# Attention and a looped mixture of experts: an earlier first load of w2, a longer lead of the given rows, nine fewer tiles turned by TensorE

## The chip, the cores and the metric

The kernel runs on one core of a Trainium2 chip, in one launch, in fp32. The metric is the device time of one execution in microseconds, as the median of repeated runs. The names of the engines in the profile: PE is TensorE (matmuls; PEld its weight loads), DVE is VectorE, ACT is ScalarE, POOL is GpSimd, SP is SyncE, which here only issues DMAs. A name with q (SPq) is an engine's sequencer, which issues and waits.

## The reference, cut to what matters

The input x is 2 sequences of 2048 tokens with 256 dimensions, 4096 tokens in all.

```
x = x + layernorm(attention(layernorm(x)))        # one head of 128, rotary positions
z = layernorm(x)
for _ in range(2):                                # LOOPS
    z_norm = rmsnorm(z) * norm_w
    scores = softmax(z_norm @ router_w)           # 8 experts
    the two largest scores, divided by their sum, are the weights of two experts
    z = z + sum over both: weight * ((silu(z_norm @ w1[e]) * (z_norm @ w3[e])) @ w2[e])
x = x + layernorm(z)                              # w1, w3: 256 x 512, w2: 512 x 256 per expert
```

The second loop's routing needs the first loop's results, token by token.

## The kernel before, in words

**Stages.** First the projections of x (to about 83 us in the profiled execution), then the attention (to about 410 us), then the experts: 71 tiles of 128 token rows for each loop, 142 in one sequence (a short end follows, in which the results of loop 1 are summed and normed). All the order of the work is written out by hand in Python, and each engine executes its own instructions in that order. An instruction that waits holds up everything behind it on its engine, and a DMA that waits holds up everything behind it on the queue that issues it.

**Attention.** A loop over `step` computes a block of scores in each step. For the first sequence (`EXCHANGED`) the exponentials are moved into turned blocks by DMAs on SP (`move_chunks`, L1449, tile `wall<-pr`, sixteen for each pair of query tiles) and VectorE turns them within blocks (`turn_chunks`, tile `pt`). In between, `extend(e)` (L1375 and on) works out for each expert the product of w2 with the router's weights: four DMAs on SP bring w2 into `wb`, four VectorE transposes make `wT`, eight small matmuls make `tp_e`. In the loop `p` numbers the pairs of query tiles and `a` runs from 0 to 7 within one; `p = -1` is the lead-in of the pipeline. `extend` is begun, which issues its four DMAs, at `a == NS - 3`, that is 5, of the pair before the one in which it is used.

**The expert tiles.** `slot(m, beside, size)` puts down the work around tile m. A tile passes these steps, each several slots apart:

- `gather` (GpSimd, indirect DMA): 128 rows of `zd` into `xg`, two tiles to a buffer. It needs the list `token`, which the routing ends with.
- `keep` (SP): a pair of tiles is written to DRAM, `xs<-xg`. `load` (SP): four DMAs bring it back with its blocks exchanged, `xb<-xs`. Both are left out for a *direct* tile.
- `turned`, two slots ahead of the matmuls: VectorE turns `xb` within blocks (`xT<-xb`). For a direct tile TensorE turns `xg` with two matmuls against the identity (`tp_x`, L1011) and ScalarE copies the result (L1012).
- `hidden`: eight records of matmul on TensorE, `p` (L1025), and ScalarE's silu, `a` (L1034). `gate`: VectorE's product `g` (L1039), and its DMA `gd<-g` on SP (L1044).
- `hidden_back`, once for two tiles: four DMAs `gb<-gd` on SP (L1051). `turn_hidden`: VectorE's `gT`. `mix`, five slots after `hidden`: the matmuls `py` (L1067).
- `give`: ScalarE's evacuation `y` (L1080), and GpSimd's indirect DMA to `given` (L1081), where each token finds its two rows.

The PSUM pool of `py` and `tp_x` has two banks; that of p has two for `p1` and three for `p3`.

**Which tiles are direct** is a list of ranges (loop, first, end), with NX = 71:

```
DIRECT = ((0, 54, NX), (1, 0, 2), (1, 12, 30), (1, 54, NX))
```

**Routing beside the tiles.** The tokens of a loop are in two groups, the first of 18 blocks of 128, the second of 14. `before` of a group of loop 1 first takes up the results of loop 0 (`logits`): `load_given` issues a DMA of 528 KB on SP for two blocks (L316, `given<-given`), `add_first` has ScalarE multiply the second rows (L337) and VectorE add the first rows to z (L338), `add_second` has GpSimd add the rest (L344). Then logits, softmax, the two largest, the positions and the lists follow, mostly on VectorE. Such a routine is a generator whose `yield` gives its cost in units. `advance` runs it beside the tiles with a budget of 16 or 17 units for each slot, in two halves, one ahead of `hidden` and `mix` and one behind them (SLOT = 16, HALF = 8). So a yield of 8 puts what comes behind it half a slot later.

Of the kernel before, what the change touches and what calls it, by code (L numbers as in the profile page):

```python
# [29 lines left out]
def attn_moe_kernel(  # L30
# [21 lines left out]
    E, _, F = w1.shape  # L52
# [13 lines left out]
    NX = TOP_K * T + E - 1  # L66
# [162 lines left out]
    def load_expert(e):  # L229
        a = ND * F  # L230
        for j, w in enumerate((w1, w3)):
            nc.sync.dma_start(
                out=wall[:, e, j * a : (j + 1) * a].rearrange("p (c f) -> p c f", c=ND),
                in_=by_dims(w[e]),
            )
        spread(wall[:, e, 2 * a :].rearrange("p (c d) -> p c d", c=NF)[:, :, :D], w2[e], NF)
# [33 lines left out]
    SLOT, HALF = 16, 8  # L270
# [5 lines left out]
    class Turn:  # L276
# [116 lines left out]
        def logits(self):  # L393

            n = self.n
            last = self.loop - 1
            nc.vector.tensor_copy(self.z[:, :, D:Z], raw[:, self.ts, :])
            y = {}
            yield SLOT
            for i in range(2):  # L400
                y[i] = self.load_given(last, i, nc.sync)
                yield HALF
            ms = rpool.tile([P, NM], F32, tag="fl_sd", name="ms")[:, :n]
            rms = rpool.tile([P, NM], F32, tag="fl_sh", name="rms")[:, :n]
            lg = self.lg.rearrange("p e t -> p t e")
            done, parts = 0, []

            for i in range(n // 2 + 5):
                if i + 2 < n // 2:
                    y[i + 2] = self.load_given(last, i + 2, nc.sync)  # L410
                if parts and parts[0][0] == i - 2:
                    _, part = parts.pop(0)
                    w = part.stop - part.start
                    nc.vector.tensor_tensor(
                        lg[:, part, :],
                        self.z[:, part, D:Z],
                        rms[:, part].rearrange("p (t o) -> p t o", o=1).to_broadcast([P, w, E]),
                        ALU.mult,
                    )

                    nc.vector.tensor_copy(self.z[:, part, D], rms[:, part])
                if 0 <= i - 3 < n // 2 and ((i - 3) % 3 == 2 or i - 3 == n // 2 - 1):
                    part = slice(done, 2 * (i - 2))
                    parts.append((i, part))
                    done = part.stop
                    w = part.stop - part.start
                    nc.vector.tensor_scalar(
                        ms[:, part], rms[:, part], 1.0 / D, RMS_EPS, ALU.mult, ALU.add
                    )
                    nc.gpsimd.tensor_tensor(rms[:, part], ms[:, part], neg_half[:, :w], ALU.pow)  # L430
                if 0 <= i - 2 < n // 2:
                    for t in range(2 * i - 4, 2 * i - 2):
                        sq = rpool.tile([P, D], F32, tag="sq", name="sq")
                        nc.scalar.activation(
                            sq, self.z[:, t, :D], AF.Square, accum_out=rms[:, t : t + 1]
                        )
                if 0 <= i - 1 < n // 2:
                    self.add_second(i - 1, y.pop(i - 1))
                if i < n // 2:
                    self.add_first(last, i, y[i])  # L440
                yield 6 if i >= n // 2 else 10 if self.g == 0 else 12
            assert not parts and not y

        def store(self, i):
# [493 lines left out]
    TURN = 2  # L938


    DIRECT = ((0, 54, NX), (1, 0, 2), (1, 12, 30), (1, 54, NX))
    BACK = 4
    LAG = 5

    class Job:


        def __init__(self, loop, i):
# [3 lines left out]
            self.first = self.second = None  # L952
            self.direct = any(l == loop and lo <= i < hi for l, lo, hi in DIRECT)

# [401 lines left out]
    NS = NT // 2  # L1356
    LEAD = NS + 1
    LATER = 6
    with tc.tile_pool(name="prob", bufs=6, **left) as pprob, tc.tile_pool(
# [44 lines left out]
        def score(u):  # L1404
            t, c = divmod(u, NKC)
            b, qi = divmod(t, NT)
            if c == 0:
                nms[t] = small.tile([P, NKC], F32, tag="m4", name="m4")
            sc[u] = ps_s.tile([P, KC], F32, tag="sc", name="sc")
            nc.tensor.matmul(  # L1410
                sc[u],
                lhsT=qkT[b][:, 0, qi * P : (qi + 1) * P],
                rhs=qkT[b][:, 1, c * KC : (c + 1) * KC],
                start=True,
                stop=True,
            )
            nc.vector.tensor_reduce(nms[t][:, c : c + 1], sc[u], AX.X, ALU.min)  # L1417
            if c == NKC - 1:
                nm = small.tile([P, 1], F32, tag="nm", name="nm")
                nc.vector.tensor_reduce(nm, nms[t], AX.X, ALU.min)  # L1420
                nms[t] = nm

        def exponents(u):
            t, c = divmod(u, NKC)
            if c == 0:
                s4s[t] = small.tile([P, NKC], F32, tag="s4", name="s4", bufs=6)
            p, i = divmod(t, QG)
            if i == 0:
                prs[p, c] = pprob.tile([P, QG, KC], F32, tag="pr", name="pr")
            nc.scalar.activation(  # L1430
                prs[p, c][:, i],
                sc.pop(u),
                AF.Exp,
                bias=nms[t],
                scale=-1.0,
                accum_out=s4s[t][:, c : c + 1],
            )
# [7 lines left out]
        def move_chunks(p, c):  # L1445

            pr = prs.pop((p, c))
            for a in range(4):
                nc.sync.dma_start(  # L1449
                    out=standing(p)[32 * c : 32 * (c + 1), :, a], in_=pr[32 * a : 32 * (a + 1)]  # L1450
                )
# [121 lines left out]
        for step in range(NS * NP + LEAD + LATER + 1):  # L1573
            u = chunks.get(step - NKC - 1)
            if u is not None and u // (NT * NKC) in EXCHANGED:
                t, c = divmod(u, NKC)
                p, i = divmod(t, QG)
                if i == QG - 1:
                    move_chunks(p, c)
            u = chunks.get(step - NKC)  # L1580
            if u is not None:
                exponents(u)
            p, a = divmod(step - LEAD - LATER, NS)
            if 0 <= p < NP:
                (turn_chunks if p // (NP // B) in EXCHANGED else transposes)(p, a)
            for gen in list(leaving):
                if next(gen, True):
                    leaving.remove(gen)
            if (p, a) >= (ROUTED + 1, 1):
                credit = min(credit, 0) + STEP  # L1590
                while credit > 0:
                    took = next(first, None)
                    if took is None:
                        break
                    credit -= took
                if credit > 0:
                    for m in itertools.islice(ahead, 1):
                        fetch_rows(m)
            u = chunks.get(step)
            if u is not None:  # L1600
                score(u)
            if a == 0 and 0 < p <= NP:
                values(p - 1, NS - 1)
                leaving.append(leave(p - 1))
                next(leaving[-1])
                if p == NP // B:

                    bigs[0].close()
                    rpool = ctx.enter_context(tc.tile_pool(name="route", bufs=1, **right))
                    spool = ctx.enter_context(tc.tile_pool(name="rows", bufs=2, **right))  # L1610
            if 0 <= p < NP:
                for g in WHEN.get(a, ()):
                    values(p, g)
            if a == NS // 2 and HELD <= p - NP // B + HELD < E:
                load_expert(p - NP // B + HELD)
                nc.gpsimd.tensor_copy(
                    extended(p - NP // B + HELD), ext[:, p - NP // B, :, :]
                )
            if a == NS - 3 and -1 <= p < E - 1:
                extending = extend(p + 1)  # L1620
                next(extending)
            elif 0 <= p < E and a < NS - 3:
                next(extending)
            e = p if p < NP // B else p - 1 - NP // B + HELD
            if (0 <= p < HELD or p > NP // B) and e < E:
                if a == 2:
                    scaling = scale_expert(e)
                    next(scaling)
                elif a == 5:
                    next(scaling)  # L1630
# [116 lines left out]
```

## Time and profile before

| | us |
|---|---|
| median of 3 runs | 1220.25 |
| lowest and highest of them | 1219.07, 1220.92 |
| profiled execution, its own time | 1223.01 |
| its span, first to last instruction | 1221.2 |
| mean granted TensorE clock, as a share of full speed | 0.981 |

The profile is of one execution. Of each engine it tells the busy time, for groups of equal instructions the count and mean duration, and for the idle time ahead of an instruction what ended it (its releaser). The chain of waits follows the execution back from its last instruction to what released each step. All times of day in what follows are microseconds from the span's start. Which wait counts must be read in the stretch where it lies: a busy share of the whole span is a mean over stages with different limits.

### The profile page before, as it was taken

What the parts mean: (1) busy time and instruction counts of PE and PEld (TensorE: products, weight loads), DVE (VectorE), ACT (ScalarE), POOL (GpSimd) and SP (SyncE); (2) the same over time, 40 slices, a digit from 0 to 9 for tenths busy, and PEclk for the clock granted to TensorE, in tenths of its full rate; (3) what the DMA queues carried; (4) which work ended last, traced back from release to release, by engine and by line L of the source; (5) the groups of instructions that cost most, each with busy time, mean ns of one, the idle gap of its engine ahead of it and who ended that gap; (6) DMA issues with size and microseconds to landing.
All of it is one profiled execution on the core that took longest, in us unless ns stands there. A gap on an engine that the chain in (4) does not pass through costs nothing.

```text
span 1221.2 us, 16498 instructions
## 1 busy us (share of the span) xinstructions
PE 1150.9 (94%) x4082; PEld 709.6 (58%) x4082; DVE 655.2 (54%) x1707; ACT 423.9 (35%) x967; POOL 627.1 (51%) x1011
## 2 busy tenths in 40 slices
PE   6986999899989799999999999998999999999985
PEld 4543666566766455555555566555666555566554
DVE  5645788767797368433333558224673333367314
ACT  4443333235545222222222642223522222244314
POOL 3560485555422444455444773554744554478573
PEclk9988999999999899999999999999999999999988
DMA  4715688725301588798877966588765897888755
GB/s 147 215 36 128 148 204 196 180 87 155 96 26 53 139 229 218 197 236 237 217 203 214 275 185 175 164 234 246 225 182 148 232 253 218 232 268 250 209 169 185
DMA packets 232169, 226.25 MB, mean 185 GB/s; under 512 B 83280, under 2 KB 179408, under 8 KB 232080
## 3 DMA queue, kind: packets, MB, share of 16 engines
q1 hardware_dynamic: 208592, 161.08, 48.6%
q0 software_dynamic: 20752, 60.97, 17.8%
q10 hardware_dynamic: 2736, 3.16, 0.8%
q8 instruction: 39, 0.64, 0.2%
q14 instruction: 50, 0.41, 0.1%
HBM read 123.82 MB, written 84.52 MB: 171 GB/s over the span
## 4 chain that ended last, share of the span: by engine, by line
PE 58%; DMA 4%; issue 2%; SPq 2%; DVE 1%; ACT 0%; POOL 0%; ACTq 0%; DVEq 0%; POOLq 0%
PE p L1025 37%; PE py L1067 19%; DMA given<-given 1%; PE tp_x L1011 1%; SPq L995 1%; DMA gd<-g 1%; DMA gb<-gd 1%; PE sum L917 1%; DMA xg<-zd,token 1%; SPq L1051 0%; DMA zd<-y 0%; DMA xs<-xg 0%; PE ps_l L665 0%; DVE ln_st L198 0%; DMA given<-y,to 0%
## 5 line engine op out<-in xcount | busy, mean ns | idle before, releaser
L1025 PE MATMUL p<-wall,xT 128*128 x1136 | 515.2, 597 | 6.7 <-ACT a L1034 5.0
L1025 PEld LDWEIGHTS p<-wall,xT 128*128 128x128 f32 x1136 | 212.7, 192 | 220.7 <-issue 210.0
L1081 POOL DMA_INDIRECT given<-y,to x142 | 143.9, 1013 | 301.5 <-ACT y L1080 212.2
L1067 PE MATMUL py<-wall,gT 128*128 x1136 | 274.2, 385 | 5.8 <-issue 5.8
L1067 PEld LDWEIGHTS py<-wall,gT 128*128 128x128 f32 x1136 | 217.4, 192 | 98.0 <-issue 70.5
L1039 DVE TENSOR_TENSOR g<-a,p 128x512 f32<-128x512 f32 x142 | 97.2, 685 | 270.3 <-issue 226.6
L1080 ACT ACTIVATE y<-py,rms 128x264 f32<-128x264 f32 (+1 forms) x142 | 67.5, 475 | 337.2 <-PE py L1067 318.7
L966 POOL DMA_INDIRECT xg<-zd,token x142 | 142.3, 1002 | 33.0 <-issue 24.3
L1034 ACT ACTIVATE a<-p,rms 128x512 f32<-128x512 f32 x142 | 97.3, 685 | 157.2 <-PE p L1025 106.1
L1410 PE MATMUL sc<-qkT 128*128 128x512 f32 x256 | 134.5, 620 | 11.9 <-ACT pr L1430 11.1
L263 DVE STREAM_TRANSPOSE gT<-gb 128x512 f32<-128x512 f32 x142 | 100.1, 706 | 67.4 <-DMA gb<-gd 66.6
L1482 PE MATMUL po<-pt,v 128*128 128x256 f32 x512 | 129.9, 388 | 1.9 <-DVE pt L1456 1.6
L1482 PEld LDWEIGHTS po<-pt,v 128*128 128x128 f32 x512 | 98.5, 194 | 53.6 <-issue 35.2
L1430 ACT ACTIVATE pr<-sc,nm 128x512 f32<-128x512 f32 x128 | 87.6, 690 | 97.2 <-DVE nm L1420 63.4
L1417 DVE TENSOR_REDUCE m<-sc 128x1 f32<-128x512 f32 x128 | 87.7, 686 | 37.4 <-PE sc L1410 37.1
L185 POOL TENSOR_TENSOR rds<-rs_v,neg_half 128x2 f32<-128x2 f32 (+1 forms) x24 | 19.8, 824 | 95.3 <-DVE rs_v L184 94.7
L1410 PEld LDWEIGHTS sc<-qkT 128*128 128x128 f32 x256 | 45.6, 197 | 31.8 <-ACT pr L1430 20.6
L1456 DVE STREAM_TRANSPOSE pt<-wall 128x512 f32<-128x512 f32 x64 | 43.8, 685 | 9.3 <-DMA wall<-pr 8.4
L263 DVE STREAM_TRANSPOSE xT<-xb 128x256 f32<-128x256 f32 x88 | 35.7, 407 | 20.8 <-DMA xb<-xs 20.8
L1253 PE MATMUL pm<-wqkvT,hT 128*128 128x392 f32 x128 | 46.5, 507 | 0.0
L243 POOL TENSOR_SCALAR wall<-wall,nwp 128x1024 f32<-128x1024 f32 x16 | 45.8, 2863 | 0.2
L1469 PE MATMUL tp_p<-ident,pr 128*128 128x128 f32 x256 | 40.2, 276 | 5.0 <-ACT pr L1430 3.6
(270 smaller groups left out, 1133.6 us busy)
## 6 DMA issues: line engine op xcount, KB each, us to landing
gd<-g SPq DMA_DIRECT2D x142, 256.0 KB
gb<-gd SPq DMA_DIRECT2D x284, 128.0 KB
wall<-pr SPq DMA_DIRECT2D x128, 128.0 KB
xs<-xg SPq DMA_DIRECT2D x44, 257.0 KB
xb<-xs SPq DMA_DIRECT2D x176, 64.0 KB
given<-given SPq DMA_DIRECT2D x16, 528.0 KB
wall<-in_L_ffn_w SPq DMA_DIRECT2D x16, 512.0 KB
z<-zd POOLq DMA_DIRECT2D x32, 256.0 KB
```

The lines of the kernel that those rows point to most:

```text
L263: nc.vector.transpose(out=dst.rearrange("p c (a t) -> p a c t", t=32), in_=src.rearrange(f"p (a {columns}) -> p a c d", a=4, c=dst.shape[1]),)
L966: i = nc.gpsimd.indirect_dma_start(out=self.xg[:, k, :], out_offset=None, in_=zd[self.loop][: (SPLIT if self.i < WHOLE else T) * P, :], in ...
L1025: nc.tensor.matmul(ps, lhsT=self.xT[:, c, :], rhs=wall[:, bass.ds(self.e, 1), o : o + F].rearrange("p o f -> p (o f)"), start=(c == 0), st ...
L1034: nc.scalar.activation(self.a, p1, AF.Silu, scale=self.rms)
L1039: nc.vector.tensor_tensor(g, self.a, self.p3, ALU.mult)
L1067: nc.tensor.matmul(py[:, :w], lhsT=self.gT[:, f, :], rhs=wall[:, bass.ds(self.e, 1), o : o + w].rearrange("p o d -> p (o d)"), start=(f == 0),
L1080: nc.scalar.mul(y, self.py, self.rms)
L1081: i = nc.gpsimd.indirect_dma_start(out=given[self.loop], out_offset=bass.IndirectOffsetOnAxis(ap=self.row(self.turn.to), axis=0), in_=y, i ...
L1410: nc.tensor.matmul(sc[u], lhsT=qkT[b][:, 0, qi * P : (qi + 1) * P], rhs=qkT[b][:, 1, c * KC : (c + 1) * KC], start=True, stop=True,)
L1417: nc.vector.tensor_reduce(nms[t][:, c : c + 1], sc[u], AX.X, ALU.min)
L1430: nc.scalar.activation(prs[p, c][:, i], sc.pop(u), AF.Exp, bias=nms[t], scale=-1.0, accum_out=s4s[t][:, c : c + 1],)
L1482: nc.tensor.matmul(pos[p], lhsT=vn[p * QG // NT][:, 2 * g + j, :HD], rhs=pt[:, j, :], start=(g == 0 and j == 0), stop=(g == NS - 1 and j = ...
```

## The change

Three places, in the words of the code:

1. `logits`: one more `yield HALF` between the first two loads of given rows and the first sum, and a cost of 11 instead of 12 for each step of the second group. The two loads keep their place, and the work behind them is put down half a slot later.
2. `DIRECT`: nine tiles (3 + 2 + 4) are no longer direct. They are 68 to 70 of loop 0, 0 and 1 of loop 1, and 26 to 29 of loop 1. For them `tp_x` and its copy go, and one `xs`, four `xb` for each pair and a VectorE transpose for each tile come.
3. `extend(0)` is begun at `a == 0` of `p == -1` instead of at `a == 5`: five steps earlier. Its four DMAs then stand ahead of the first sixteen `wall<-pr` on SP's queue and not behind them. The later ones stay.

```diff
             for i in range(2):
                 y[i] = self.load_given(last, i, nc.sync)
                 yield HALF
+            yield HALF
...
-                yield 6 if i >= n // 2 else 10 if self.g == 0 else 12
+                yield 6 if i >= n // 2 else 10 if self.g == 0 else 11
...
-    DIRECT = ((0, 54, NX), (1, 0, 2), (1, 12, 30), (1, 54, NX))
+    DIRECT = ((0, 54, 68), (1, 12, 26), (1, 54, NX))
...
-            if a == NS - 3 and -1 <= p < E - 1:
+            if a == (NS - 3 if p >= 0 else 0) and -1 <= p < E - 1:
                 extending = extend(p + 1)
                 next(extending)
```

In the built order of the instructions this shows as follows. On ScalarE the first two multiplications of given rows in the second group stand behind the next `a` and not ahead of it, and the next two behind the next `y`. On VectorE each new `xT` stands behind a pair of `g` and `gT` and ahead of the next such pair. On SP the `xs` and `xb` of the tiles that open loop 1 stand directly behind each other, ahead of a `gb`, two `gd` and the following `xs`; the same holds for tiles 28 and 29 of loop 1.

## The prediction

> **What bounds the kernel now.** Read first the page, then TensorE's own waits, then the chain of waits in the stretches where TensorE idles, then the timeline there.
>
> ```profile
> span 1221.2 us, 16498 instructions
> PE 1150.9 (94%) x4082; PEld 709.6 (58%) x4082; DVE 655.2 (54%) x1707; ACT 423.9 (35%) x967; POOL 627.1 (51%) x1011
> PE p L1025 37%; PE py L1067 19%; DMA given<-given 1%; PE tp_x L1011 1%; SPq L995 1%; DMA gd<-g 1%; DMA gb<-gd 1%; PE sum L917 1%; DMA xg<-zd,token 1%; SPq L1051 0%; DMA zd<-y 0%; DMA xs<-xg 0%; PE ps_l L665 0%; DVE ln_st L198 0%; DMA given<-y,to 0%
> ...
> PE tp_x L1011 <- ACT y L1080: 3.1, 1, 3.1
> ```
>
> TensorE carries it: 94% busy, the expert tiles (p, py) 56% of the chain. So an instruction taken from TensorE inside the expert loop is worth its full length, as long as nothing else is late there. In the loop the chain of waits shows the price of a tile whose rows TensorE turns:
>
> ```profile
> 677.40 3.43 PE p L1025 x8
> 680.83 1.78 PE py L1067 x8
> 682.61 0.23 PE tp_x L1011 x2
> ```
>
> A tile takes 3.43 + 1.78 = 5.21 us, and 0.23 more when it is direct. But between 786 and 834 us the chain runs not through TensorE but through SP's queue and its transfers:
>
> ```profile
> 786.82 3.85 DMA xg<-zd,token
> 793.85 5.19 DMA gb<-gd
> 800.60 6.10 DMA gd<-g
> 824.41 3.34 DMA gd<-g
> 834.08 9.51 DMA given<-given
> ```
>
> It ends in the one stall of TensorE inside the loop. The timeline there (start, length, engine, what; in brackets idle time before it and its releaser):
>
> ```profile
> 823.54 0.71 DVE L263 STREAM_TRANSPOSE gT<-gb 128x512 f32<-128x512 f32 x1 [4.13 <-DMA gb<-gd]
> 824.43 1.94 PE L1067 MATMUL py<-wall,gT 128*128 x8
> 839.97 1.89 PE L1067 MATMUL py<-wall,gT 128*128 x8
> 841.03 0.92 ACT L337 ACTIVATE given<-given,gains 128x264 f32<-128x264 f32 x2 [8.98 <-DMA given<-given]
> 844.44 0.45 ACT L1080 ACTIVATE y<-py,rms 128x256 f32<-128x256 f32 x1
> 844.95 0.50 PE L1011 MATMUL tp_x<-ident,xg 128*128 128x128 f32 x2 [3.09 <-ACT y L1080]
> 847.66 0.92 ACT L337 ACTIVATE given<-given,gains 128x264 f32<-128x264 f32 x2 [1.25 <-DMA given<-given]
> ```
>
> ScalarE waits 9 us for the first given rows; the PSUM evacuation y stands behind that, and TensorE behind y. Also to be seen: gT is ready at 824.25, py takes it at 824.43. TensorE was within 0.2 us of waiting for SP's chain although it did not wait.
>
> **Part A, first load of w2.** Its four DMAs (2.23 us of SP) leave the place behind sixteen moves of probabilities and stand ahead of them. They wait for the last projection work (84.6 us on GpSimd, end of the qk sums); SP is otherwise idle until 99.39, and no bytes moved in that stretch, so they cost nothing; the sixteen moves still start when ScalarE's first exponentials release them.
>
> ```profile
> 109.99 2.23 SPq L252 DMA_DIRECT2D wb<-in_L_ffn_w  x4
> 115.20 0.45 DVE L1383 STREAM_TRANSPOSE wT<-wb 128x256 f32<-128x256 f32 x1 [1.81 <-DMA wb<-in_L_ffn_w]
> 120.80 0.19 PEld L1482 LDWEIGHTS po<-pt,v 128*128 128x128 f32 x1 [0.24 <-DVE pt L1456]
> ```
>
> VectorE's 1.81 us goes. Late next is TensorE itself: from 114.26 to 124.8 it stands idle for only 0.24 us on VectorE. Bounds 0 and -1.8; I take **-0.2**, the wait that ends on TensorE.
>
> **Part B, given rows.** In the program's order the first two loads keep their place on SP (behind the same gd). What moves is the sum: ScalarE's first two multiplications pass behind the next a, the next pair behind the next y. The loads land at about 841.0, 843.6 and 847.7 (the three multiplications' waits), one every 2.5 us or more. So the waits are not removed, but a and y no longer stand behind each. Step by step, in before's time: a, due at 833.3 (1.9 after its p began at 831.37), no longer waits; first multiplications 841.03 to 841.95; y to 842.4, so tp_x at 842.45 instead of 844.95 and p at 842.95 instead of 845.74. The next evacuation still stands behind the third load: it ends at 848.95; py, which needs that bank, runs 848.95 to 850.8, tp_x, and the following p starts at 851.3 instead of 852.9: **-1.6**. The 3.09 us idle turns into 0.6 and some 2.5.
>
> Here the clock matters. The granted clock in 844 to 852 was 0.81 and 0.76, and after the stall one tile took 7.18 us instead of 5.39: 1.8 lost. In the trace 2.00 us idle before 350.35 is followed by po matmuls of 634 ns instead of 379 (granted clock of 350 to 375: 0.93), while after 1.93 us before 243.8 matmuls keep their 592. The Trainium skill ("TensorE: Matmul & The Clock Gate", "What's actually happening") puts the drop to half after an idle window of about 3.4 us, freely placed. By that rule 2.5 us never costs, the sum of this part stays -1.6; by the rows it may. The trace decides: I add half of 1.8, so **-0.7**, bounds -2.5 and +0.5.
>
> The first group's sum (at about 680 us) also moves half a slot; tiles there keep their 5.44, nobody waits on TensorE before or after: 0. The later group's interval of 11 for 12, seven times, gives back 7 of the 8 units; its routing ends one unit later, 1/16 of a slot, hidden as its gathers stand behind a give in any case: 0.
>
> **Part C, direct tiles.** The ranges lose 3 + 2 + 4 = 9 tiles: loop 0's last three, loop 1's first two, loop 1's 26 to 29. TensorE gives up 9 x 0.23 = 2.1 us, ScalarE nine copies of 0.36. Added: nine VectorE transposes of 0.40, and on SP five xs (0.5) and twenty xb issues (0.61 each).
>
> Loop 1's 26 to 29: four tiles, -0.9. The last two are gathered only once routing has ended: gather 932.3, landed 936.8 at the latest (GpSimd's wait), xs 2.8 (938.76 to 941.58 in a quiet stretch), the four xb ready 5.2 to 6.4 after the first issue, so turned at 945 to 946, wanted at 945.5. I keep **-0.9**, bounds -0.9 and +0.5.
>
> Around 772 to 790 it is five tiles, -1.15 by TensorE alone. But the pair that opens loop 1 goes gather, xs, xb, transpose, in one line, and both in-order queues stand behind it: on SP gb, two gd and the next xs; on VectorE the next g and gT behind xT. Working (TensorE 0.46 earlier by then): second gather issued 774.9, landed 778.4 (3.15 to 3.85 in the chain); xs landed 781.9 (2.8 to 4.2); xT from 787.7; g 0.7 later; gd 788.8; the next xs 789.2, landed about 792.9; its xb can issue then, where before it issued at 791.23. SP's chain slips **1.7** (-0.7 to +4). The tile itself is turned at 788.1 and wanted at 788.65. From there every step of the chain is SP or transfer, so the slip is handed on to the gT at 823.54; crowded steps (gd 6.10 against 3.34 later) let it shrink, I say to 0.8. TensorE had 0.2 to spare: it comes out at **+0.6**, not -1.15. A second rule speaks the other way: "DMA: Bandwidth & Descriptors", "Anatomy of one DMA", prices a DMA at about 2.0 us plus bytes at 436 GB/s. By it (an estimate) xs is 2.6 and a 64 KB xb 2.2, the line ends 3 us sooner, nothing slips, and the part is -1.15. The row of 4.20 for xs speaks against; I take the rows.
>
> **Sum.** -0.2 - 0.7 - 0.9 + 0.6 = **-1.2**. The profiled execution took 1223.0 (span 1221.2, 1.8 around it), 2.8 above the median 1220.25; the difference is taken off the median: **1219.0**. About 0.2%, 2.4 us, can be told from no change here.
>
> **Rivals.** *SP's chain does not slip* (the moved pair's bytes fall in 776 to 784, where transfers are at 0.42 to 0.69 of their time): then -1.15 stays, no half-clock window follows the shorter idle: -0.2 - 1.6 - 0.9 - 1.15 = -3.9, 1216.4. For: that free stretch. Against: in-order g and gd behind xT.
>
> *The opening pair of loop 1 stalls TensorE.* Place: xT on VectorE before g, 787 to 793. At a slip of 3 instead of 0.8 TensorE comes out +2.8; waits of 2 us or more in one place drop the clock, +1.8; the sums then meet rows as late as before, part B 0: +2.8 + 1.8 - 0.9 - 0.2 = +3.5, 1223.8. It decides from a slip of about 2.0 (the sum is then zero), and to a loss that can be told with the clock drop. For: landings of 5 to 6 us from 793 on. Against: those come with the burst of before, which the change spreads.
>
> *The loads' move does nothing* because SP and not the sum is late: part B 0, sum -0.5, 1219.8; inside the forecast's range.
>
> **How the numbers follow.** Forecast 0.50 (own range 1217.0 to 1221.3; 0.10 of it faster by over 0.2%, 0.38 within, 0.02 slower), first rival 0.24 (faster), second 0.22 (0.20 slower, 0.02 within), others 0.04 (0.01 faster, 0.03 slower). Faster 0.35, within 0.40, slower 0.25. Range 1215.2 to 1224.0: it takes in both rivals and their bounds.
>
> **What would show it.** Right: wT's wait gone and 114 to 125 unchanged on TensorE; SP's first xb after the opening pair at 792 to 794; tp_x after the given rows' wait with under 1 us idle, one further idle of about 2.5; tiles 26 to 29 at 5.16. Wrong: idle of TensorE over 1 us between 786 and 806, or a lower granted clock there (second rival); that xb at or before 791 (first rival); py near 849 not waiting for y (part B mis-sized).

## The result, and the profile after

| | before | after |
|---|---|---|
| median of 9 runs each, us | 1219.07 | 1225.71 |
| lowest to highest, us | 1215.47 to 1223.26 | 1220.99 to 1231.83 |
| ratio after to before, 95% interval | | 1.0051 (1.0030 to 1.0072) |
| profiled execution: span, us | 1221.2 | 1228.5 |
| mean granted clock | 0.981 | 0.978 |

The change made the kernel slower by 6.2 us, give or take 2.5. The forecast was 1.2 us faster, with a range that ended at 1224.0.

The page of the changed kernel: the span, the busy times, and the chain by line.

```profile
span 1228.5 us, 16498 instructions
PE 1152.5 (94%) x4064; PEld 708.7 (58%) x4064; DVE 663.0 (54%) x1716; ACT 422.8 (34%) x958; POOL 628.2 (51%) x1011
PE p L1026 30%; PE py L1068 16%; DMA gb<-gd 2%; SPq L996 1%; SPq L1052 1%; DMA xg<-zd,token 1%; DMA gd<-g 1%; POOL xg L967 1%; POOL given L1082 1%; DMA xs<-xg 1%; PE tp_x L1012 1%; PE sum L918 1%; DVE gT L263 0%; DVE lg L415 0%; DMA zd<-y 0%
```

TensorE is as busy as before, with 18 instructions less. But the chain that ended last runs through the expert matmuls for 46% of the span instead of 56%; in exchange it runs through SP and its transfers (`xs`, `gd`, `gb`). TensorE's own waits in the changed kernel say the same (total, times, longest):

```profile
PE py L1068 <- DVE gT L263: 8.2, 4, 5.3
PE p L1026 <- DVE xT L263: 2.6, 2, 1.6
PE py L1068 <- ACT y L1081: 2.1, 2, 1.9
PE ps_l L666 <- DVE numbers L708: 1.0, 1, 1.0
```

The wait of `tp_x` for `y`, 3.1 us before, is gone. The first, third and fourth of these lines and most of the second are new; of the first, 5.3 us is the end of the tiles, where before waited 5.4.

**The pair that opens loop 1**, in the timeline of the changed kernel (SP, VectorE, TensorE):

```profile
786.82 2.53 SPq L996 DMA_DIRECT2D xb<-xs  x4
791.57 1.68 SPq L1045 DMA_DIRECT2D gd<-g  x2
793.36 3.73 SPq L982 DMA_DIRECT2D xs<-xg  x2
800.10 2.54 SPq L996 DMA_DIRECT2D xb<-xs  x4
...
791.87 0.45 DVE L263 STREAM_TRANSPOSE xT<-xb 128x256 f32<-128x256 f32 x1 [9.52 <-DMA xb<-xs]
796.51 0.40 DVE L263 STREAM_TRANSPOSE xT<-xb 128x256 f32<-128x256 f32 x1
804.95 0.45 DVE L263 STREAM_TRANSPOSE xT<-xb 128x256 f32<-128x256 f32 x1 [6.84 <-DMA xb<-xs]
810.35 0.71 DVE L263 STREAM_TRANSPOSE gT<-gb 128x512 f32<-128x512 f32 x1 [4.38 <-DMA gb<-gd]
...
805.54 3.67 PE L1026 MATMUL p<-wall,xT 128*128 x8 [1.57 <-DVE xT L263]
811.21 1.13 PE L1068 MATMUL py<-wall,gT 128*128 x4 [2.00 <-DVE gT L263]
```

VectorE stands 9.5 us at the pair's first `xT`; the second of the two `gd` (issued at 792.92) waits for a `g` behind it; the next `xs` stands behind this `gd` on SP, and 6.7 us pass from there to the next `xb`. TensorE waits at tile 73 (1.57 us) and at the next `py`, and a stretch in which TensorE was granted half its clock (a half-clock window, 812.3 to 815.7 in the clock's records) follows.

**Tiles 28 and 29 of loop 1** (m = 99, 100). SP and TensorE in the changed kernel:

```profile
938.53 0.32 SPq L982 DMA_DIRECT2D xs<-xg  x1
946.83 0.38 SPq L982 DMA_DIRECT2D xs<-xg  x1
954.27 0.54 SPq L982 DMA_DIRECT2D xs<-xg  x1
...
994.68 1.97 PE L1068 MATMUL py<-wall,gT 128*128 x8 [0.81 <-DVE gT L263]
1112.21 3.40 PE L1068 MATMUL py<-wall,gT 128*128 x8 [1.90 <-ACT y L1081]
...
1109.90 1.10 ACT L787 ACTIVATE z<-z,ln_nb,ln_rstd 128x256 f32<-128x256 f32 x2 [5.66 <-DVE ln_nb L206]
1111.70 0.46 ACT L1081 ACTIVATE y<-py,rms 128x256 f32<-128x256 f32 x1
```

The `xs` leave at the times of before (938.8, 944.2, 951.4) or up to 2.9 us later, but in before they belong to a pair later. From here the rows of every tile come one step later, up to tile 124. The wait at 1112.21 is where that ends. VectorE had stood 5.2 us at a `gT` of 1085.3, waiting for late `gb`, with the sums of the last layer norm behind it; GpSimd's `ln_rstd` then waited 4.5 us for these sums and stayed late, to the one of 1107.86, which ScalarE's `z` needs; and `y` stands behind `z`. Another half-clock window follows (1112.6 to 1116.0).

**What went as forecast.** The first load of w2 is issued at 85.92 and `wT` waits for nothing. And ScalarE's sums of given rows no longer hold up TensorE:

```profile
85.92 1.90 SPq L252 DMA_DIRECT2D wb<-in_L_ffn_w  x4
113.48 0.43 DVE L1384 STREAM_TRANSPOSE wT<-wb 128x256 f32<-128x256 f32 x1
...
844.46 0.93 ACT L337 ACTIVATE given<-given,gains 128x264 f32<-128x264 f32 x2 [1.13 <-DMA given<-given]
846.03 0.48 ACT L1081 ACTIVATE y<-py,rms 128x256 f32<-128x256 f32 x1 [0.65 <-PE py L1068]
846.97 0.92 ACT L337 ACTIVATE given<-given,gains 128x264 f32<-128x264 f32 x2 [0.47 <-DMA given<-given]
849.26 1.89 PE L1068 MATMUL py<-wall,gT 128*128 x8
```

A milestone table shows where the profiled execution loses its 7.3 us: start of `p` of a tile (m), after minus before.

| m | 0 | 53 | 67 | 71 | 75 | 82 | 97 | 102 | 124 | 131 | span |
|---|---|---|---|---|---|---|---|---|---|---|---|
| us | +3.5 | +3.8 | +5.5 | +3.2 | +9.4 | +3.7 | +3.0 | +2.8 | +4.1 | +7.9 | +7.3 |

The first 3.5 us lie in the attention. Between 71 and 75 it loses 6 us, gets 5.7 back by 82 (the stall of before at 844.95, with its half clock, that it does not have), and loses 5 us between 102 and 131.

### The profile page after: what moved, and what is told of

It reads as the page before. It is cut to its first block, busy times and chain, and to the rows that moved or that the text cites. A ratio compares the mean times of both kernels' runs of the same rounds, so it can differ in the third digit from the quotient of the medians.

```text
span 1228.5 us, 16498 instructions
## 1 busy us (share of the span) xinstructions
PE 1152.5 (94%) x4064; PEld 708.7 (58%) x4064; DVE 663.0 (54%) x1716; ACT 422.8 (34%) x958; POOL 628.2 (51%) x1011
## 4 chain that ended last, share of the span: by engine, by line
PE 47%; DMA 6%; issue 5%; DVE 3%; SPq 3%; POOL 2%; ACT 1%; ACTq 0%; DVEq 0%; POOLq 0%
PE p L1026 30%; PE py L1068 16%; DMA gb<-gd 2%; SPq L996 1%; SPq L1052 1%; DMA xg<-zd,token 1%; DMA gd<-g 1%; POOL xg L967 1%; POOL given L1082 1%; DMA xs<-xg 1%; PE tp_x L1012 1%; PE sum L918 1%; DVE gT L263 0%; DVE lg L415 0%; DMA zd<-y 0%
## 5 line engine op out<-in xcount | busy, mean ns | idle before, releaser
L263 DVE STREAM_TRANSPOSE xT<-xb 128x256 f32<-128x256 f32 x97 | 39.8, 411 | 42.9 <-DMA xb<-xs 42.3
```

The lines of the kernel that those rows point to most:

```text
L263: nc.vector.transpose(out=dst.rearrange("p c (a t) -> p a c t", t=32), in_=src.rearrange(f"p (a {columns}) -> p a c d", a=4, c=dst.shape[1]),)
```

## The experiments

All ratios are to executions of before on the same chip in the same comparison, with 95% intervals. Four chips were used, and before's median was 1219.4 to 1223.7 us on them. Single executions scatter by about 3 us around their median, so a ratio settles some 0.15%, and a trace settles which wait there was. *Spare time* below is the start of `p` minus the end of its `xT`, from the trace.

### The parts alone

First load of w2 alone (the edit of `extend`), in two comparisons:

```diff
-            if a == NS - 3 and -1 <= p < E - 1:
+            if a == (NS - 3 if p >= 0 else 0) and -1 <= p < E - 1:
```

> Before with only the first load of w2 moved. In the changed kernel the expert loop began 3.5 us later than before (its first p at 413.4 instead of 409.9), all of it lost between 165 and 260 us. Theory 1 (the forecast: the load is hidden, the 3.5 us is run-to-run scatter of the attention): the time within 1 us of before, ratio 0.999 to 1.001. Theory 2 (the moved load shifts VectorE's later work in the attention): +2 to +4 us, ratio 1.002 to 1.003, and the first p of the loop again at 412 to 414.

Measured: 0.9995 (0.9973 to 1.0016), first `p` at 409.0.

> Before with only the first load of w2 moved, once more. Theory 1 (hidden, no effect): ratio 0.999 to 1.001. Theory 2 (it is what was left of the loss): ratio 1.001 to 1.003.

Measured: 1.0001 (0.9980 to 1.0022). No effect that can be told; the two intervals leave room for some 2 us either way. The 3.5 us of the attention lie inside the scatter: in the 13 profiles without the moved load the first `p` came between 407.8 and 415.7 (mean 411.9), in the 7 with it between 409.0 and 417.6 (mean 413.7). A loss of up to some 2 us is not ruled out.

Given rows alone:

```diff
+            yield HALF
...
-                yield 6 if i >= n // 2 else 10 if self.g == 0 else 12
+                yield 6 if i >= n // 2 else 10 if self.g == 0 else 11
```

> Before with only the given rows' sums moved (half a slot more, interval 11 for 12). Theory 1 (the forecast): the 3.09 us wait of TensorE at tp_x splits into under 1 us and some 2.5 us; -2.5 to +0.5 us, ratio 0.998 to 1.0. Theory 2 (in the changed kernel that stall vanished only because TensorE was already 9 us late there, so alone the move only shifts the wait): 0 to +1 us. Theory 3 (the move takes the stall and its half-clock window away whole): -4 to -5.5 us, ratio 0.9955 to 0.997.

Measured: 1.0017 (1.0002 to 1.0033): slower, with its median beyond all three theories. Its trace has no stall at `tp_x`, and `py` behind the third load waits 1.2 us for `y`, where the forecast had 2.5; the later stretch, tiles 71 to 82, took 58.95 us for 63.16. What it paid lies earlier, at the first group's sums, where TensorE waited for the lists that the routing ends with. TensorE, then VectorE:

```profile
757.00 0.47 PE L1012 MATMUL tp_x<-ident,xg 128*128 128x128 f32 x2
758.22 0.40 PE L666 MATMUL ps_l<-numbers,rows 128*128 128x86 bf16 x6 [0.75 <-DVE numbers L708]
759.03 1.55 PE L1026 MATMUL p<-wall,xT 128*128 x3 [0.41 <-issue]
...
757.41 0.43 DVE L705 TENSOR_TENSOR numbers<-numbers,high 128x258 bf16<-128x258 bf16 x1
757.87 0.29 DVE L708 TENSOR_SCALAR numbers<-numbers,low 128x258 bf16<-128x258 bf16 x1
758.08 0.95 DVE L700 TENSOR_TENSOR rows<-within,column 128x768 bf16<-128x768 f32 x1
```

Half a slot later, two steps of the lists fall into one half of a slot: VectorE makes `rows` and `numbers` twice in a row, and the second `ps_l` wants what is ready only at 758.16. Tiles 53 to 67 took 80.4 us for 78.5. In the six profiles with this edit, a tile there (m = 55) always took 0.36 to 0.56 us longer, and the tile at the lists (m = 64) 0.3 to 1.8 us more than the 6.07 of before in five of the six. Tiles 53 to 67 together took 78.5 to 81.5 us, so the price differs between executions.

The move in the second group alone (the interval of 11 stays) tests that:

```diff
+            if self.g == 1:
+                yield HALF
```

> The given rows' sums moved half a slot in the second group alone (the additional HALF only there, interval 11 for 12); the first group keeps its times. In the run with both groups moved, TensorE waited 0.75 us for the first group's lists (ps_l, waiting for VectorE's numbers at 758 us) and tiles 60 to 67 took 1.6 us longer. Theory 1 (the loss of the given rows' part is the first group's): that wait is gone, tiles 60 to 71 take 63.6 us again as before, tiles 71 to 82 about 59 us, and the time is within 0.1% of before or up to 2 us below: ratio 0.998 to 1.0005. Theory 2 (the second group's move costs): ratio 1.001 to 1.003 as with both moved.

Measured: 1.0005 (0.9989 to 1.0020). The wait for the lists is gone and tiles 53 to 67 take 78.5 us again:

```profile
752.79 0.40 PE L667 MATMUL ps_l<-numbers,rows 128*128 128x86 bf16 x6
753.03 0.47 PE L1013 MATMUL tp_x<-ident,xg 128*128 128x128 f32 x2
753.34 0.40 PE L667 MATMUL ps_l<-numbers,rows 128*128 128x86 bf16 x6
```

The wait is shown to be the first group's. That the whole 1.7 thousandths are, is only likely: the intervals of the two versions touch. There was no gain either, and the reason is in the profiles of other experiments, which have before's code in this stretch. Six such executions are before, `a_only`, `a_again`, `c_mid`, `m_last2` and `m_first2`. TensorE's wait at this place was 3.1 us in before and

```profile
PE tp_x L1011 <- ACT y L1080: 1.8, 1, 1.8
```

in `a_only`, 0.4 in `c_mid`, and there was none of `tp_x` in the other three (`py` waited for `y` 0.2 to 0.5). The stall that the change was to remove was the longest of six, and only before and `a_only` had a half-clock window behind it; 3.1 us and half clock are not what this place costs in the mean.

Tiles 26 to 29 of loop 1 alone, and the five tiles at the loops' border alone:

```diff
-    DIRECT = ((0, 54, NX), (1, 0, 2), (1, 12, 30), (1, 54, NX))
+    DIRECT = ((0, 54, NX), (1, 0, 2), (1, 12, 26), (1, 54, NX))      # c_mid
+    DIRECT = ((0, 54, 68), (1, 12, 30), (1, 54, NX))                 # c_open
```

> Before with only loop 1's tiles 26 to 29 not direct. Theory 1 (read from the changed kernel's trace): direct tiles are where SP's and VectorE's rows get ahead again; without these four, rows of the tiles after 30 come with 2 to 6 us to spare instead of 8 to 10, and py waits for gT until the next direct tiles: +1 us of waits near 990 to 1040 and, if a wait comes near 2 us at 1110 with a half-clock window, +3 to +5 us in all, less the 0.9: ratio 1.002 to 1.004. Theory 2 (the forecast): TensorE is never late, -0.9 us, ratio 0.999.

Measured: 1.0018 (1.0001 to 1.0034). Tiles 86 to 131 took 242.97 us; the profiles with before's code there took 238.9. TensorE in `c_mid`:

```profile
976.57 1.97 PE L1067 MATMUL py<-wall,gT 128*128 x8 [0.66 <-DVE gT L263]
989.28 3.65 PE L1067 MATMUL py<-wall,gT 128*128 x8 [2.15 <-DVE gT L263]
```

The mechanism of the changed kernel, in other tiles. The second wait is followed by a half-clock window.

> Before with only loop 0's last three tiles and loop 1's first two not direct. Theory 1 (read from the changed kernel's trace): the opening pair's rows stand in SP's and VectorE's queues, TensorE waits over 1 us twice between 800 and 815 and loses a half-clock window (together about 6 us), and then does not meet the wait for the given rows near 845 (3.1 us and 1.8 us of half clock); net +0.5 to +2.5 us, ratio 1.0005 to 1.002. Theory 2 (the forecast): no wait over 1 us there, +0.6 us. Theory 3: both stalls stand, +4 to +6 us, ratio 1.0035 to 1.005.

Measured: 1.0025 (1.0008 to 1.0041), waits of 1.69 us at tile 71 and 1.07 at tile 73 for `xT`, and 1.84 at a `py`; no half-clock window there, which Theory 1 had expected. Against before's profile its tiles 60 to 82 are 3.1 us shorter, since it lacks the stall at 844; against the other five executions of before's code there (121.6 to 126.2 us, `c_open` 123.6) it is in their middle. One profile does not carry the sign; the ratio does.

### Which pair it is

> Before with only loop 1's tiles 28 and 29 not direct (the pair whose rows are gathered across the end of the routing, at 907 and 935 us). Theory 1 (this pair is the loss: its xs cannot leave before 938 us, and every later pair stays one step late in SP's queue): tiles 97 to 131 take about 182.5 us for 177.7, ratio 1.001 to 1.0035, spare time ahead of p from tile 101 on 2 to 6 us. Theory 2 (all four count alike, each one a bit of lost catching up): half of the loss, +2 us of the 4.8 in that stretch. Theory 3 (the other two are the loss): -0.46 us.

> Before with only loop 1's tiles 26 and 27 not direct; 28 and 29 stay direct. Theory 1 (28 and 29 are the loss): TensorE is not late, tiles 86 to 131 take 0.46 us less than before (238.5 for 238.9), ratio 0.9985 to 1.0005. Theory 2 (all four count alike): +2 us there, ratio 1.001 to 1.002.

In `DIRECT` the first (`m_last2`) has `(1, 12, 28)` for `(1, 12, 30)`, the second (`m_first2`) has `(1, 12, 26), (1, 28, 30)` for it. Spare time in us:

| m | before | m_first2 | m_last2 | c_mid | after |
|---|---|---|---|---|---|
| 97 | 10.2 | 8.6 | 10.0 | 8.4 | 8.4 |
| 99 | 9.8 | 9.8 | 1.5 | 1.8 | 2.2 |
| 100 | 9.6 | 9.6 | 4.0 | 3.1 | 4.0 |
| 102 | 8.9 | 9.0 | 2.5 | 2.3 | 2.4 |
| 106 | 9.6 | 10.2 | 4.8 | 1.6 | 1.9 |

The lateness is tiles 28 and 29 alone, as the first theory said; 26 and 27 leave next to no trace. What follows in time is less plain, and both first theories missed it: tiles 97 to 131 took 177.5 us in `m_last2` and not 182.5, and both kernels measured 1.0013 (1.0000 to 1.0027, 1.0000 to 1.0026), and in neither profile did TensorE wait between 940 and 1125; both saved their 0.46 us there. With spare time of 2 to 5 us the lateness is a risk and not yet a wait. Why `m_first2` is not faster stays open at the size of its interval. The lateness turned into waits in some profiles and not in others: tiles 86 to 131 lost 4.1 us in `c_mid` and 4.3 in after, and next to nothing in `m_last2` and `after_keep_open`, which are as late. And the ratio of `c_mid` is only just clear of 1.

> Before with only loop 1's tiles 0 and 1 not direct; loop 0's last three stay direct. Theory 1 (the loss at the loops' border is this pair: its rows are gathered and must go through xs, xb and xT in the time the tile has): TensorE waits for xT at tiles 71 and 73 (spare time ahead of p under 1 us, where it was 10.8 and 2.7), waits of 1 to 4 us in all between 785 and 812, ratio 1.001 to 1.003. Theory 2 (it is the three tiles of loop 0, whose transfers crowd the queues just before): spare time at 71 stays over 3 us, ratio 0.999 to 1.0005.

> Before with only loop 0's tiles 68 to 70 not direct; loop 1's first two stay direct. Theory 1 (the loss is loop 1's opening pair): tiles 67 to 71 take 0.5 to 2 us less, no wait for xT at 71, ratio 0.9985 to 1.0005. Theory 2 (the loss is these three): ratio 1.001 to 1.003 and waits of TensorE over 1 us between 785 and 812.

The edits: `(1, 0, 2)` taken out; `(0, 54, 68)` for `(0, 54, NX)`. Measured: `o_pair` 1.0034 (1.0018 to 1.0049), `o_end3` 1.0006 (0.9991 to 1.0021). TensorE in `o_pair`:

```profile
795.59 3.67 PE L1025 MATMUL p<-wall,xT 128*128 x8 [1.69 <-DVE xT L263]
809.12 3.67 PE L1025 MATMUL p<-wall,xT 128*128 x8 [2.86 <-DVE xT L263]
813.81 2.02 PE L1067 MATMUL py<-wall,gT 128*128 x8 [1.02 <-DVE gT L263]
```

The opening pair is the loss. Loop 0's last three bring nothing of their 0.7 us, and in the profile of `o_end3` waits of 1.1 us at `tp_x` and 0.5 at the `p` behind it, which before has too (0.7 and 0.4), were followed by a half-clock window.

### Do the parts add up

The edit of the first keeps `(1, 12, 30)`, of the second `(0, 54, NX), (1, 0, 2)`, of the third has `(0, 54, 68), (1, 0, 4), (1, 12, 30)`, each in the changed kernel.

> The changed kernel with loop 1's tiles 26 to 29 direct again, the rest of the change kept. Theory 1 (losses stand in separate stretches and add up): the 4.3 us of tiles 86 to 131 come back and the rest stays: ratio to before 1.001 to 1.003. Theory 2 (the opening pair's lateness alone is the loss and is handed on to the end): nothing comes back, ratio 1.004 to 1.006.

Measured: 1.0064 (1.0034 to 1.0094), from seven executions. The trace gives the 4.3 us back (tiles 86 to 131 in 238.93, no wait there), the time does not: the clearest miss of these expectations. But the trace is of the fastest of the seven (1220.55 us for a median of 1227.43), so it does not show what the others lost. The sum of the parts that it keeps (0 + 1.7 + 2.5) lies inside its interval.

> The changed kernel with loop 0's last three and loop 1's first two tiles direct again; w2's load, the given rows and tiles 26 to 29 stay changed. Theory 1 (the parts add up: given rows 1.7, tiles 26 to 29 1.8 thousandths, w2 nothing): ratio 1.0015 to 1.0055, no wait for xT at tiles 71 and 73, spare time from tile 99 on still 1.5 to 6 us. Theory 2 (the loss needs the opening and the later lateness together): ratio 0.999 to 1.001.

Measured: 1.0031 (1.0011 to 1.0050). No wait for `xT` at tiles 71 and 73; spare time from tile 99 to 111 1.6 to 6.3 us. As the parts add up.

> The changed kernel with loop 1's tiles 0 to 3 and 26 to 29 direct (loop 0's last three not). Theory 1 (both places of lateness are closed; what is left is the first group's wait for its lists, +1 to +2 us, against the 2 to 3 us that direct tiles 2 and 3 gave): ratio 0.998 to 1.001. Theory 2 (moving w2's load and the given rows costs by itself in another way): ratio 1.002 to 1.005.

Measured: 1.0023 (1.0011 to 1.0035). Both places of lateness are closed, TensorE's waits between 430 and 1150 us are 1.2 us at the longest, and it is still slower than before, beyond what Theory 1 allowed. The given rows' 1.7 would be enough to explain it, if tiles 2 and 3 gave nothing here, but its profile does not show them: from `p` of tile 0 to `p` of tile 131 it took 698.9 us, where before took 703.5. Its first `p` came at 415.1, so the moved load of w2 is a rival as well. What it lost by stays open.

> The changed kernel once more, for a second execution in profile and a closer ratio. Theory 1 (the lateness after tile 100 is there in every execution, the stalls that it becomes are chance): spare time ahead of p again 2 to 6 us from tile 100 to 124, and 0.1 to 2 us at tiles 71 to 74; waits of TensorE in other places than in the first profile; ratio 1.003 to 1.007. Theory 2 (each stall is fixed): waits at the same tiles (py of tiles 68, 102 and 124, p of tile 73) with the same lengths within 0.5 us.

Measured: 1.0120 (1.0089 to 1.0151), on a chip where before took 1222.59 us. TensorE in this second profile of the changed kernel:

```profile
796.83 3.67 PE L1026 MATMUL p<-wall,xT 128*128 x8 [1.43 <-DVE xT L263]
811.38 4.51 PE L1026 MATMUL p<-wall,xT 128*128 x6 [3.88 <-DVE xT L263]
...
967.26 1.97 PE L1068 MATMUL py<-wall,gT 128*128 x8 [0.74 <-DVE gT L263]
989.20 1.10 PE L1068 MATMUL py<-wall,gT 128*128 x4 [1.06 <-DVE gT L263]
...
1118.86 3.26 PE L1068 MATMUL py<-wall,gT 128*128 x8 [2.74 <-ACT y L1081]
```

The same lateness (spare time 0.1 at tiles 71 and 73, 1.5 to 6 from 99 to 124), other and longer waits. From `p` of tile 0 to `p` of tile 131 the two profiles of the changed kernel took 707.9 and 714.6 us, before 703.5, and the seventeen other profiles 697.8 to 704.1: most of what these two lost lies in the expert tiles. In both the lateness came with the program; why its price differs that much between executions is not shown. Alone the parts make 0 + 1.7 + 1.8 + 2.5 = 6.0 thousandths, for 5.1 (3.0 to 7.2) and 12.0 (8.9 to 15.1) of the whole: that they add up holds for the first comparison, and in the second something more is lost.

### The other direction

If direct tiles are where rows get ahead again, more of them at the loops' border should help.

```diff
-    DIRECT = ((0, 54, NX), (1, 0, 2), (1, 12, 30), (1, 54, NX))
+    DIRECT = ((0, 54, NX), (1, 0, 4), (1, 12, 30), (1, 54, NX))
```

> Before with two more direct tiles, 2 and 3 of loop 1 (the other direction). Theory 1 (a direct tile at the loops' border gives SP's queue the time of an xs and four xb back): spare time ahead of p at tiles 73 to 80 grows from 2 to 4 us to over 5 us, waits between 785 and 852 become rarer; +0.46 us of TensorE against some 2 us of waits in the mean: ratio 0.9975 to 1.0005. Theory 2 (given rows, not tile rows, end the wait at 844 and TensorE's 0.46 us is all that is left): ratio 1.0 to 1.002.

Measured: 0.9978 (0.9963 to 0.9994).

> Before with loop 1's tiles 2 and 3 direct too, once more. Theory 1 (the gain is the waits between 785 and 852 that spare time of 7 to 10 us at tiles 73 to 80 takes away): ratio 0.996 to 0.9995 again, tiles 60 to 82 at 121 to 122 us. Theory 2 (it was chance): ratio 0.9995 to 1.001.

Measured: 0.9994 (0.9978 to 1.0010), on another chip: here the gain cannot be told from nothing. Spare time in us:

| m | before | o_pair | d_more | d_more_again |
|---|---|---|---|---|
| 71 | 10.8 | 0.1 | 10.9 | 11.0 |
| 73 | 2.7 | 0.1 | 9.9 | 9.9 |
| 76 | 2.3 | 3.3 | 8.1 | 8.1 |
| 78 | 1.6 | 2.3 | 6.8 | 7.2 |
| 80 | 1.6 | 3.9 | 7.6 | 6.9 |

Two tiles for 0.46 us of TensorE lift the spare time by 5 to 7 us for eight tiles. Tiles 60 to 82 took 121.4 and 121.5 us, at the lower end of before's 121.6 to 126.7.

> Before with loop 1's tiles 2 to 5 direct too. Theory 1 (spare time is needed only up to what four direct tiles give; two more cost TensorE 0.46 us and bring nothing): ratio 0.9965 to 1.0, 0.2 to 1 us above four direct tiles. Theory 2 (more spare time goes on bringing something): below four direct tiles by over 0.5 us.

Measured: 1.0007 (0.9995 to 1.0020), above what Theory 1 allowed. No gain over four (0.9994 in the same comparison) is seen; whether six cost anything, the intervals do not settle.

> Before with loop 1's tiles 2 and 3 direct too and the given rows' sums half a slot later in the second group alone. Theory 1 (the given rows' move costs only through the first group, and the waits between 785 and 852 are closed by the direct tiles): ratio 0.997 to 0.9998, no half-clock window between 430 and 1150 us, tiles 60 to 82 at 121 to 122 us. Theory 2 (the second group's move costs too): ratio 1.0 to 1.002.

Measured: 0.9964 (0.9951 to 0.9978), median 1218.16 for 1223.72 us: this version beats before and the changed kernel. It has two more direct tiles and the given rows' move in the second group alone. TensorE's waits in it between 430 and 1150 us are

```profile
PE tp_x L1013 <- DMA xg<-zd,token: 0.9, 1, 0.9
PE py L1069 <- issue: 0.5, 1, 0.5
PE p L1027 <- issue: 0.4, 1, 0.4
```

and no half-clock window begins in that time, although this was the slowest of its 22 executions (1223.74 us; its first `p` came late, at 415.5). The closed waits are shown; how much of the 0.36% each of the two edits brings is not.

## Why the prediction was wrong

**First load of w2, forecast -0.2.** Right as far as it can be told.

**Given rows, forecast -0.7, measured +2.1 (0.2 to 4.0).** Two steps failed. "The first group's sum also moves half a slot; ... nobody waits on TensorE before or after: 0" looked at the sums and not at what stands behind them in the same routine: the lists, on which TensorE itself waits. That cost 1.9 us in the profile of `b_only`. And the gain was sized by one stall of one execution, which six executions show at 0.2 to 3.1 us. The working at the second group itself was right in form: `tp_x` no longer waits, and `py` waits for the `y` behind the third load, 1.2 us in `b_only` and 0.4 in `b_late` for the forecast's 2.5.

**Tiles 26 to 29, forecast -0.9 with bounds -0.9 and +0.5, measured +2.2 (0.1 to 4.1).** The working asked whether these tiles themselves come in time, and they do, with 1.5 to 4 us to spare. It did not ask what their `xs` and `xb` take from the tiles behind them. The term that was put at nothing is this lateness: 1.5 to 6 us of spare time from tile 99 to 124 of the changed kernel, where before has 7 to 11, and in `c_mid` waits and half clock that made tiles 86 to 131 4.1 us longer. The bound was set too narrow for that reason; the sign was wrong.

**The border of the loops, forecast +0.6, measured +3.0 (1.0 to 5.0).** The order of the waits was right, and the failed term is the slip of SP: put at 1.7 us, with a bound of 4. Counted from the start of `p` of tile 67, SP's first `xb` after the pair came 24.6 us later in before, and 28.0 to 30.2 later in the kernels with the pair turned by VectorE: a slip of 3.4 to 5.6. Up to the `xs` ahead of it the working holds (22.6 us by its times, 21.0 to 23.8 measured). What failed is the leg from that `xs` to its `xb`: 3.7 us were put in, and it took 5.3 to 7.2. Before has 6.2 us between the two as well, but for another reason:

```profile
785.04 5.97 SPq L981 DMA_DIRECT2D xs<-xg  x2
791.23 2.53 SPq L995 DMA_DIRECT2D xb<-xs  x4
```

The line of `xs` holds two, and the second, issued at 790.69, had waited for its gather, with `xb` behind it; so that leg does not tell how long the rows took. The records of the packets tell it for the five kernels with the turned pair. The pair's own `xs` met a free queue: its rows (128 packets of 2056 bytes) began to move 0.8 us after its issue, and its `xb` came after 3.0 to 3.4. The next `xs`, issued 0.44 us behind a `gd`, began after 1.3 to 3.1 us, while the bytes of that `gd` were still moving; its last packet left at 2.8 to 5.2, and 2.0 to 3.5 more passed until the `xb`. Why this last piece was longer as well (0.6 to 1.6 for the pair's own) is not shown. The working counted `gb` and `gd` as issues on SP, and not the time that their bytes take ahead of the rows. It also had the pair's first tile turned 0.55 us before it was wanted; TensorE waited 1.69 us for it in `c_open` and in `o_pair`, and it had 0.7 to spare in after. The price by the Trainium skill ("DMA: Bandwidth & Descriptors", "Anatomy of one DMA"), an estimate of 2.6 us, would have missed by more; that section gives it for DMAs issued by GpSimd, and these are issued by SP. Point and place of the second rival were right (it decides from a slip of about 2.0), and so was its sign: TensorE stood idle for 1.57 us before 805.54. It had a chance of 0.22. It left out that tiles 26 to 29 would be late as well, so that even its 1223.8 was too low.

**The clock.** The half added for a wait of 2.5 us was reasonable. The Trainium skill ("TensorE: Matmul & The Clock Gate", "What's actually happening") speaks of an idle window of some 3.4 us; here less was enough: waits of 1.84 us (`a_only`), 1.90 (after) and 2.15 (`c_mid`) were followed by half clock, while one of 2.86 (`o_pair`) and one of 2.21 (`after_keep_open`) were not. The length of a wait does not decide it, but its place nearly does. In each trace all half-clock windows begin on one grid of 3.41 us, and what separates the cases is how long TensorE was idle between two points of the grid. Over the 20 traces, from 430 to 1150 us, with the ends of matmuls as the profile models them: all six grid intervals with 2.0 us of idle time or more were followed by half clock, two of the six with 1.61 to 1.98, and none with less. The 2.86 us of `o_pair` fell into two intervals, as 0.88 and 1.98. By these figures (an estimate, for a limit of 2.0) a wait of 2.5 us at a random place has a chance of 0.56.

## What to carry to other kernels

A part that costs the busiest engine 0.23 us each may be what lets two in-order queues catch up; before taking it away, read the spare time of the tiles behind it and not only its own. A stall seen once is one draw: look for the same stretch in other executions before it is booked as a gain. And a routine moved by half a slot moves its last step too, so ask who waits for that.

## What the runs showed of the hardware

Lateness without a wait has a price that differs between executions: one program, with nearly the same spare time, lost 0.5% in one comparison and 1.2% in another, on a chip where before took 3.5 us longer too. Half-clock windows between 430 and 1150 us (eight in the 20 traces) lasted 3.41 us each. A wait is followed by one according to how much of it falls between two points of a 3.41 us grid, in these traces always from 2.0 us on and never below 1.6. And a DMA that SP has issued is not yet moving: with a `gd` issued 0.44 us ahead of it, an `xs` began to move 1.3 to 3.1 us after its issue in five kernels, on a free queue after 0.8.
